# Third edge pass of a graph network: groups of edges taken in pairs

## The chip, the cores and the metric

The kernel runs on one core of one Trainium2 chip. The metric is the device time of one execution in microseconds (us). The core's engines work in parallel, each through its own list of instructions in order: PE (TensorE, matmuls), DVE (VectorE), ACT (ScalarE), POOL (GpSimd, which issues the gathers here) and SP (SyncE, which issues the plain loads). They wait for one another by semaphores. SBUF is the core's on-chip memory, PSUM the memory into which PE writes and from which DVE and ACT can read[...].

## The reference

A graph with 30,000 nodes of 128 features and 960,000 edges, sorted by destination, goes through two layers. The first is a relational convolution in two rounds; it takes the first and second pass over the edges. The second layer is the one that the change touches. For each of four edge types t:

```
k = x @ Wk[t] + bk[t];  q = x @ Wq[t] + bq[t];  v = x @ Wv[t] + bv[t]
eta = sigmoid(k[dst] + q[src])
msg = where(edge_type == t, eta * v[src], 0)
agg = segment_sum(msg, dst);  outs.append(agg + x @ Ws[t] + b[t])
```

and the layer's output is the mean over t, added to x. An edge has one type, so each edge needs one row k[dst, type], one q[src, type] and one v[src, type], one sigmoid and one product of 128 values, and a sum by destination. All is fp32.

## The kernel before, in words

The kernel makes three passes over the edges. The first two (functions named c1 and c2) compute the first layer; node tables for the second layer are made beside the second. Between and beside them, finished nodes are worked on in small steps. The third pass, named g, has its body in `gate_body`; only this function is changed.

A pass is a loop of 25 iterations (`NI`). An iteration has 100 groups (`NG`), a group three tiles of 128 edges (`G` = 3, `TP` = 128), five groups (`S`) are a superblock, and 25 groups a stage, for which the lists of source rows and of relative destinations are loaded at once (`loads`). As the edges are sorted, the destinations of a group lie in a window of 32 nodes.

The instructions stand on each engine as the program writes them (`manual_schedule`); nothing is reordered. For group n the third pass does this:

- `window(n)`, L555: SP loads 128 rows of the table of k that can occur in the group (`kw`, ten buffers, L560). It is called five groups ahead.
- `types(s)`, L551, and `onehot(s)`, L562: SP loads the codes of a superblock; DVE makes from them, by comparison, a one-hot matrix `oh` (128 x 1920, L564) that picks the row of k for each edge, and `sel` (128 x 480, L570) that picks the destination for each edge. `onehot(s + 1)` stands in group 1 of each superblock.
- `gather`, L118: POOL issues three indirect DMAs per group into `qv[n]`, each 128 rows of 256 values, q and v side by side. There are ten buffers of a group, so the gathers of group n wait until group n-10 has been used up.
- `keys(n)`, L574: three matmuls of `oh` and `kw` write k for 384 edges into `pk[n]`, one PSUM bank (four buffers).
- L618: DVE adds q to `pk[n]` in place; L619: ACT takes the sigmoid in place.
- `sums(n)`, L581: DVE multiplies `pk[n]` with v into `msg` (L586, three buffers); three matmuls (L588) sum the messages of the group by destination into `po[s]`.
- `add_windows`, L410 to L413: DVE adds the five windows of a superblock to the aggregate `agg` in SBUF. It stands in group 4 of the next superblock.
- `after_third`, L751 to L772: copies, transposes and stores finished nodes (`c`, `pr`, `o`).

The order within group n is: loads, gathers of n, `keys(n + 1)`, the addition and sigmoid of n, `sums(n - 2)`, and then, where they fall due, `onehot` and `add_windows`:

```
if n + 1 < NG:
    keys(n + 1)
nc.vector.tensor_add(pk[n], pk[n], qv[n][:, :, 0, :])
nc.scalar.activation(pk[n], pk[n], AF.Sigmoid)
if n > 1:
    sums(n - 2)
```

So on DVE the product of group n-2 comes directly behind the addition of group n, and PE alternates between three matmuls of keys and three of sums. The gathers of group n stand in POOL's list without any work of other engines between, so POOL can run ahead as far as the ten buffers of `qv` allow. At a stage's start, every 25 groups, `stage_boundary` stands in the program, and `leave_stage` ten groups later.

Of the kernel before, what the change touches and what calls it, by code (L numbers as in the profile page):

```python
# [9 lines left out]
F32 = mybir.dt.float32  # L10
I32 = mybir.dt.int32
BF16 = mybir.dt.bfloat16
AF = mybir.ActivationFunctionType
# [6 lines left out]
P = 128  # L20
D = 128
# [9 lines left out]
TP = 128  # L31
NT = E // TP
G = 3
GE = G * TP
W = 32
NGR = NT // G
S = 5
SB = 5
NQ = 4
NS = NQ * SB  # L40
NGS = S * SB
NTS = NGS * G
NG = S * NS
# [6 lines left out]
NX = N + LAG  # L50
LEAD = 3 * VB
GAP = 8
EPS = 1e-5
CH = 5
PX, KX = 120, 10
# [17 lines left out]
def kernel(  # L73
# [29 lines left out]
    nc = tc.nc  # L103
# [7 lines left out]
    qvtab = nc.dram_tensor("qvtab", (NX * T, 2 * D), F32, kind="Internal").ap()  # L111
# [5 lines left out]
    def gather(to, table, idx):  # L117
        nc.gpsimd.indirect_dma_start(  # L118
            out=to, out_offset=None, in_=table,
            in_offset=bass.IndirectOffsetOnAxis(ap=idx, axis=0))  # L120
# [23 lines left out]
    eps = consts.tile([P, 1], F32, name="eps")  # L144
    nc.vector.memset(eps, EPS)

# [188 lines left out]
    def sorted_path():  # L335
# [5 lines left out]
        with ExitStack() as all_:  # L341
# [40 lines left out]
            def leave_stage():  # L382

                for engine in ENGINES:
                    tc.previous_stage_wait(engine)

            def stage_tile(io, name, array, dt, i, k, more=0):

                t = io.tile([TP, NTS + more], dt, name=name)
                nc.sync.dma_start(t, array[:, ds(i * (NQ * NTS) + k * NTS, NTS + more)])  # L390
                return t

            def firsts(io, i, k):

                t = io.tile([1, 32], I32, name="firsts")
                nc.sync.dma_start(t, first_st[ds(i * NQ + k, 1), :])
                return t

            def bases(t, engine):
                _, vals = nc.values_load_multi_w_load_instructions(  # L400
                    t[:, :NGS], engines=[engine],
                    min_val=0, max_val=N - 1, skip_runtime_bounds_check_because=IN_RANGE)
                return vals

            def edge_row(row, i, s, n):

                return bass.AP(tensor=row.tensor, offset=(i * NG + s * S) * GE,
                               ap=[[0, n], [GE, S], [1, GE]])

            def add_windows(po, base, s):  # L410
                for g in range(S):
                    to = agg[:, ds(base[s % SB * S + g], W)]
                    nc.vector.tensor_add(to, to, po[:, g, :])  # L413
# [129 lines left out]
            def gate_body(i, io, pool, ps, cp, iw, ic, beside):  # L543
                stage = {}
                kb, oh, kw, sel, pk, qv, po, base, kbase = {}, {}, {}, {}, {}, {}, {}, {}, {}

                def loads(k):
                    stage[k] = [firsts(io, i, k)] + [stage_tile(io, *a, i, k) for a in (
                        ("qi", qidx, I32), ("relc", reld, F32))]

                def types(s):  # L551
                    kb[s] = pool.tile([P, S, GE], BF16, name="kb")
                    nc.sync.dma_start(kb[s], edge_row(kcode, i, s, P))

                def window(n):  # L555
                    k = n // NGS
                    if n % NGS == 0:
                        kbase[k] = bases(stage[k][0], SP)
                    kw[n] = pool.tile([P, D], F32, name="kw", bufs=10)
                    nc.sync.dma_start(kw[n], ktab[ds(kbase[k][n % NGS] * T, P), :])  # L560

                def onehot(s):  # L562
                    oh[s] = pool.tile([P, S, GE], F32, name="oh")
                    nc.vector.tensor_tensor(oh[s], kb[s],  # L564
                                            ic.unsqueeze(2).to_broadcast([P, S, GE]),
                                            ALU.is_equal)
                    sel[s] = pool.tile([TP, S * G, W], F32, name="sel", bufs=3)
                    t0 = s % SB * S * G
                    relc = stage[s // SB][2][:, t0:t0 + S * G]
                    nc.vector.tensor_tensor(  # L570
                        sel[s], iw[:TP].unsqueeze(1).to_broadcast([TP, S * G, W]),
                        relc.unsqueeze(2).to_broadcast([TP, S * G, W]), ALU.is_equal)

                def keys(n):  # L574
                    pk[n] = ps.tile([TP, G, D], F32, name="pk", bufs=4)
                    for j in range(G):
                        nc.tensor.matmul(pk[n][:, j, :],  # L577
                                         lhsT=oh[n // S][:, n % S, j * TP:(j + 1) * TP],
                                         rhs=kw[n], start=True, stop=True)

                def sums(n):  # L581
                    s, g = n // S, n % S
                    if g == 0:
                        po[s] = ps.tile([P, S, W], F32, name="po")
                    msg = pool.tile([TP, G, D], F32, name="msg", bufs=3)
                    nc.vector.tensor_mul(msg, pk[n], qv[n][:, :, 1, :])  # L586
                    for j in range(G):
                        nc.tensor.matmul(po[s][:, g, :], lhsT=msg[:, j, :],  # L588
                                         rhs=sel[s][:, g * G + j, :],
                                         start=(j == 0), stop=(j == G - 1))  # L590

                loads(0)
                types(0)
                for n in range(S):
                    window(n)
                onehot(0)
                keys(0)
                for n in range(NG):
                    s, g, k = n // S, n % S, n // NGS
                    if n % NGS == 0:  # L600
                        if n:
                            tc.stage_boundary()
                        if k + 1 < NQ:
                            loads(k + 1)
                    if g == 0 and s % SB == 2:
                        leave_stage()
                    if g == 0 and s + 1 < NS:
                        types(s + 1)
                    if n + S < NG:
                        window(n + S)  # L610
                    qv[n] = pool.tile([TP, G, 2, D], F32, name="qv", bufs=10)
                    t0 = n % NGS * G
                    for j in range(G):
                        gather(qv[n][:, j].rearrange("p a f -> p (a f)"), qvtab,
                               stage[k][1][:, t0 + j:t0 + j + 1])
                    if n + 1 < NG:
                        keys(n + 1)
                    nc.vector.tensor_add(pk[n], pk[n], qv[n][:, :, 0, :])  # L618
                    nc.scalar.activation(pk[n], pk[n], AF.Sigmoid)  # L619
                    if n > 1:  # L620
                        sums(n - 2)
                    if g == 1 and s + 1 < NS:
                        onehot(s + 1)
                    if g == 4 and s:
                        add_windows(po[s - 1], base[(s - 1) // SB], s - 1)
                    if g == 4 and s % SB == 0:
                        base[k] = bases(stage[k][0], DVE)
                    beside(n)
                sums(NG - 2)
                sums(NG - 1)  # L630
                add_windows(po[NS - 1], base[NQ - 1], NS - 1)


# [31 lines left out]
            def after_second(weights):  # L665
# [9 lines left out]
                def steps(at, pool, ps, deep):  # L675
# [6 lines left out]
                    hT = pool.tile([P, VB], F32, name="hT")  # L682
                    kt = pool.tile([VB, T, D + GAP], F32, name="kt")[:, :, :D]
                    qvt = pool.tile([VB, T, 2 * D + GAP], F32, name="qvt")[:, :, :2 * D]
                    got = {}
# [120 lines left out]
            edge_pass("c1", rel_body(h0, basis[0], False), after_first, 2, codes)  # L806
            edge_pass("c2", rel_body(h1, basis[1], True), after_second, 2)
            edge_pass("g", lambda weights: gate_body, after_third, 1)


# [230 lines left out]
```

## Time and profile before

| what | value |
|---|---|
| time, median of three runs | 33,966.85 us (33,952.1 to 33,968.91) |
| the profiled execution's own time | 34,363.18 us |
| its span, first to last instruction | 34,361.4 us |
| PE busy | 19,886.4 us, 58% |
| DVE busy | 12,399.5 us, 36% |
| ACT busy | 3,636.0 us, 11% |
| POOL busy | 21,304.2 us, 62% |
| third pass, from its first gather to its last | 22,630.1 to 34,330.1 us |
| granted TensorE clock, mean of the span | 0.675 |

The three passes compared, in stretches inside each of them (busy us):

| stretch | PE | DVE | ACT | POOL | clock | DMA share | GB/s |
|---|---|---|---|---|---|---|---|
| 200 to 11,500 | 6,415.79 | 3,933.95 | 1,009.46 | 7,063.54 | 0.74 | 0.24 | 64 |
| 11,600 to 22,500 | 6,587.65 | 4,036.69 | 1,160.89 | 7,005.11 | 0.78 | 0.25 | 65 |
| 22,700 to 34,300 | 6,679.37 | 4,180.45 | 1,318.54 | 7,022.93 | 0.51 | 0.41 | 122 |

How to read the lines of the profile that follow. A group row gives the line of the kernel, engine and operation, what it writes and reads, its shape and how often it occurs; then the busy time in us and the mean of one in ns; then how long the engine had been idle just before these instructions, with what ended most of that. A wait row names the engine and line, what ended the wait, its sum in us, how often, and the longest. A timeline row gives start and duration in us, the engine, the instruction, how many in a row it stands for (x), and in brackets the idle time ahead of it and what ended that. "issue" means that the profile shows nothing that the engine waited for, "remote" that the releaser is not among the instructions that the profile could name. Ends of matmuls are modelled, so the record of a matmul can end earlier than the matmul. The profile's own chain of the work that ended last is empty for this kernel.

### The profile page before, as it was taken

How to read it: one execution, taken by the hardware profiler on the slowest of the kernel's cores; microseconds unless marked ns; L12 is line 12 of the kernel's file. 1: busy time of each engine (PE TensorE's matmuls, PEld its weight loads, DVE VectorE, ACT ScalarE, POOL GpSimd, SP SyncE). 2: the span in 40 equal slices, each digit the busy share in tenths (PEclk: the TensorE clock that was granted, in tenths of full speed). 3: DMA queues.
4: the chain of work that ended last, by engine and by line, in shares of the span. 5: the costliest groups of instructions: out<-in, count | busy, mean ns of one | idle time of the engine just before them, and what ended most of it. 6: DMA issues, size and time to landing. Idle time of an engine off the chain costs nothing.

```text
span 34361.4 us, 321543 instructions
## 1 busy us (share of the span) xinstructions
PE 19886.4 (58%) x83304; PEld 16933.4 (49%) x83304; DVE 12399.5 (36%) x32695; ACT 3636.0 (11%) x9834; POOL 21304.2 (62%) x22514
## 2 busy tenths in 40 slices
PE   4555555555555566656656666555555555555555
PEld 3444444444444444444444444445555555555555
DVE  4333333333333333333333333333333333333333
ACT  1000000000000011111111111111111111111111
POOL 5666666666666666666666666656656666666665
PEclk7777777777777777777777777765555555555555
DMA  3222222222222222222222222234444444444443
GB/s 100 64 63 63 64 64 64 63 64 63 63 63 63 66 65 66 65 66 65 66 65 66 65 66 65 65 105 123 122 121 121 121 121 122 122 123 121 121 122 118
DMA packets 2171202, 2914.97 MB, mean 85 GB/s; under 512 B 684764, under 2 KB 1617880, under 8 KB 2169544
## 3 DMA queue, kind: packets, MB, share of 16 engines
q0 software_dynamic: 840000, 1967.52, 21.0%
q1 hardware_dynamic: 923347, 651.19, 6.5%
q10 hardware_dynamic: 406197, 276.11, 2.8%
q8 instruction: 802, 13.14, 0.2%
q14 instruction: 856, 7.01, 0.1%
HBM read 2618.79 MB, written 274.16 MB: 84 GB/s over the span
## 4 chain that ended last, share of the span: by engine, by line


## 5 line engine op out<-in xcount | busy, mean ns | idle before, releaser
L118 POOL DMA_INDIRECT hg<-h,idx x15000 | 14189.1, 946 | 8366.8 <-issue 4281.9
L520 PE MATMUL pa<-sb,hg 128*128 128x256 f32 x30000 | 9211.6, 464 | 6063.6 <-issue 3309.4
L520 PEld LDWEIGHTS pa<-sb,hg 128*128 128x128 f32 x30000 | 6897.0, 239 | 7881.0 <-issue 3785.8
L118 POOL DMA_INDIRECT qv<-qvtab,qi x7500 | 7088.1, 945 | 4658.3 <-issue 2317.6
L515 DVE SCALAR_TENSOR_TENSOR sb<-cp,relc,ce 128x256 f32<-128x256 f32 x15000 | 6132.8, 475 | 5165.4 <-remote 3864.0
L588 PE MATMUL po<-sel,msg 128*128 128x32 f32 x15000 | 3459.4, 387 | 4659.8 <-DVE msg L586 3274.0
L588 PEld LDWEIGHTS po<-sel,msg 128*128 128x128 f32 x15000 | 3417.7, 327 | 4956.1 <-DVE msg L586 3424.9
L577 PE MATMUL pk<-kw,oh 128*128 128x128 f32 x15000 | 3965.9, 438 | 332.2 <-DVE oh L564 284.4
L618 DVE TENSOR_TENSOR pk<-pk,qv 128x384 f32<-128x384 f32 x2500 | 1407.4, 563 | 7030.1 <-remote 5356.4
L524 ACT COPY ab<-pa 128x256 f32<-128x256 f32 x5000 | 1809.0, 373 | 20007.9 <-remote 10336.1
L577 PEld LDWEIGHTS pk<-kw,oh 128*128 128x128 f32 x15000 | 3460.6, 330 | 334.9 <-issue 334.9
L479 PE MATMUL po<-ab,bas 128*128 128x160 f32 x16000 | 2456.1, 308 | 275.1 <-ACT ab L524 144.6
L479 PEld LDWEIGHTS po<-ab,bas 128*128 128x128 f32 x16000 | 2381.7, 198 | 384.4 <-ACT ab L524 169.6
L413 DVE TENSOR_TENSOR agg<-agg,po 128x32 f32 x7500 | 1401.6, 187 | 2827.7 <-remote 699.9
L619 ACT ACTIVATE pk<-pk 128x384 f32<-128x384 f32 x2500 | 1185.8, 475 | 9327.1 <-DVE pk L618 5397.8
L715 PE MATMUL bank<-wall,hT 128*120 128x512 f32 x1524 | 1052.1, 814 | 1083.9 <-ACT hT L711 338.1
L586 DVE TENSOR_TENSOR msg<-pk,qv 128x384 f32<-128x384 f32 x2500 | 1368.1, 547 | 126.8 <-remote 94.6
L449 PE MATMUL cp<-coeff,oh 128*128 128x64 f32 x4000 | 693.9, 306 | 964.1 <-issue 769.6
L449 PEld LDWEIGHTS cp<-coeff,oh 128*128 128x128 f32 x4000 | 687.4, 233 | 1019.3 <-issue 902.4
L564 DVE TENSOR_TENSOR oh<-kb,cp 128x1920 f32<-128x1920 bf16 x500 | 1072.2, 2144 | 47.5 <-issue 31.9
L715 PEld LDWEIGHTS bank<-wall,hT 128*120 128x120 f32 x1524 | 346.5, 246 | 1429.1 <-issue 627.9
L726 DVE TENSOR_TENSOR kt<-bank,ball 120x512 f32<-120x512 f32 x254 | 175.7, 692 | 2336.7 <-PE bank L715 895.3
(77 smaller groups left out, 3396.7 us busy)
## 6 DMA issues: line engine op xcount, KB each, us to landing
hg<-h,idx POOLq DMA_INDIRECT x15000
kb<-kcode SPq DMA_DIRECT2D x500, 480.0 KB
kw<-ktab SPq DMA_DIRECT2D x2500, 64.0 KB
er<-in_et_row SPq DMA_DIRECT2D x2000, 64.0 KB
qvtab<-qvt ACTq DMA_DIRECT2D x254, 480.0 KB
qv<-qvtab,qi POOLq DMA_INDIRECT x7500
ktab<-kt ACTq DMA_DIRECT2D x254, 240.0 KB
ce<-ce ACTq DMA_DIRECT2D x500, 60.0 KB
```

The costliest lines, as they stand in the source:

```text
L118: nc.gpsimd.indirect_dma_start(out=to, out_offset=None, in_=table, in_offset=bass.IndirectOffsetOnAxis(ap=idx, axis=0))
L413: nc.vector.tensor_add(to, to, po[:, g, :])
L449: nc.tensor.matmul(pc[s][:, c].rearrange("p q l b -> p (q l b)"), lhsT=oh[s][:, c, :], rhs=coeff.rearrange("p q l b -> p (q l b)"), start= ...
L479: nc.tensor.matmul(po[s].rearrange("p s w -> p (s w)"), lhsT=bas[:, b, :], rhs=ab[s][:, b].rearrange("p s w -> p (s w)"), start=(b == 0), ...
L515: nc.vector.scalar_tensor_tensor(sb, iw[:TP].unsqueeze(1).to_broadcast([TP, B, W]), relc[:, t0 + j:t0 + j + 1], ce[s][:, g * G + j, :].uns ...
L520: nc.tensor.matmul(pa.rearrange("p b w -> p (b w)"), lhsT=hg[:, j, :], rhs=sb.rearrange("p b w -> p (b w)"), start=(j == 0), stop=(j == G ...
L524: nc.scalar.copy(ab[s][:, :, g, :], pa)
L577: nc.tensor.matmul(pk[n][:, j, :], lhsT=oh[n // S][:, n % S, j * TP:(j + 1) * TP], rhs=kw[n], start=True, stop=True)
L586: nc.vector.tensor_mul(msg, pk[n], qv[n][:, :, 1, :])
L588: nc.tensor.matmul(po[s][:, g, :], lhsT=msg[:, j, :], rhs=sel[s][:, g * G + j, :], start=(j == 0), stop=(j == G - 1))
L618: nc.vector.tensor_add(pk[n], pk[n], qv[n][:, :, 0, :])
L715: nc.tensor.matmul(bank(a, VB, T * D), lhsT=hT, rhs=wall[:, a].rearrange("p t f -> p (t f)"), start=True, stop=True)
```

## The change

Two neighbouring groups, n = 2m and 2m + 1, become a pair m. A pair's keys lie in one PSUM tile of two banks (`pk[m]`, two buffers[...]), its gathered rows in one `qv[m]` (five buffers of a pair), its messages in one `msg` (two buffers of a pair, by default of the pool). One addition, one sigmoid and one product work on the 768 values per partition of a pair. The matmuls and gathers stay as many; those of a pair's keys and of a pair's sums each stand together, six in a row.

The order changes too. In the second group of pair m the program has: `sums(m - 1)`, that is the product and the six matmuls of the pair before; then the keys of the next two groups; then the addition and the sigmoid of pair m. `onehot` and `add_windows` stay in groups 1 and 4 of their superblock. Windows of k are loaded seven groups ahead (`AHEAD`) and still have ten buffers. The stages begin at groups 0, 26, 50 and 76, so that a pair never crosses a boundary within the program's order, and a stage is left ten groups after it begins. The first two passes are the same.

```
--- before.py
+++ after.py
@@ -50,6 +50,7 @@
 NX = N + LAG
 LEAD = 3 * VB
 GAP = 8
+AHEAD = 7
 EPS = 1e-5
 CH = 5
 PX, KX = 120, 10
@@ -572,53 +573,62 @@
                         relc.unsqueeze(2).to_broadcast([TP, S * G, W]), ALU.is_equal)
 
                 def keys(n):
-                    pk[n] = ps.tile([TP, G, D], F32, name="pk", bufs=4)
+                    if n % 2 == 0:
+                        pk[n // 2] = ps.tile([TP, 2, 4, D], F32, name="pk")[:, :, :G, :]
                     for j in range(G):
-                        nc.tensor.matmul(pk[n][:, j, :],
+                        nc.tensor.matmul(pk[n // 2][:, n % 2, j, :],
                                          lhsT=oh[n // S][:, n % S, j * TP:(j + 1) * TP],
                                          rhs=kw[n], start=True, stop=True)
 
-                def sums(n):
-                    s, g = n // S, n % S
-                    if g == 0:
-                        po[s] = ps.tile([P, S, W], F32, name="po")
-                    msg = pool.tile([TP, G, D], F32, name="msg", bufs=3)
-                    nc.vector.tensor_mul(msg, pk[n], qv[n][:, :, 1, :])
-                    for j in range(G):
-                        nc.tensor.matmul(po[s][:, g, :], lhsT=msg[:, j, :],
-                                         rhs=sel[s][:, g * G + j, :],
-                                         start=(j == 0), stop=(j == G - 1))
-
+                def sums(m):
+
+                    msg = pool.tile([TP, 2, G, D], F32, name="msg")
+                    nc.vector.tensor_mul(msg, pk[m], qv[m][:, :, :, 1, :])
+                    for n in (2 * m, 2 * m + 1):
+                        s, g = n // S, n % S
+                        if g == 0:
+                            po[s] = ps.tile([P, S, W], F32, name="po")
+                        for j in range(G):
+                            nc.tensor.matmul(po[s][:, g, :], lhsT=msg[:, n % 2, j, :],
+                                             rhs=sel[s][:, g * G + j, :],
+                                             start=(j == 0), stop=(j == G - 1))
+
+                begins = [-(-k * NGS // 2) * 2 for k in range(NQ)]
                 loads(0)
                 types(0)
-                for n in range(S):
+                for n in range(AHEAD):
                     window(n)
                 onehot(0)
                 keys(0)
+                keys(1)
                 for n in range(NG):
                     s, g, k = n // S, n % S, n // NGS
-                    if n % NGS == 0:
+                    m = n // 2
+                    if n in begins:
                         if n:
                             tc.stage_boundary()
                         if k + 1 < NQ:
                             loads(k + 1)
-                    if g == 0 and s % SB == 2:
+                    if n - 2 * S in begins:
                         leave_stage()
                     if g == 0 and s + 1 < NS:
                         types(s + 1)
-                    if n + S < NG:
-                        window(n + S)
-                    qv[n] = pool.tile([TP, G, 2, D], F32, name="qv", bufs=10)
+                    if n + AHEAD < NG:
+                        window(n + AHEAD)
+                    if n % 2 == 0:
+                        qv[m] = pool.tile([TP, 2, G, 2, D], F32, name="qv", bufs=5)
                     t0 = n % NGS * G
                     for j in range(G):
-                        gather(qv[n][:, j].rearrange("p a f -> p (a f)"), qvtab,
+                        gather(qv[m][:, n % 2, j].rearrange("p a f -> p (a f)"), qvtab,
                                stage[k][1][:, t0 + j:t0 + j + 1])
-                    if n + 1 < NG:
-                        keys(n + 1)
-                    nc.vector.tensor_add(pk[n], pk[n], qv[n][:, :, 0, :])
-                    nc.scalar.activation(pk[n], pk[n], AF.Sigmoid)
-                    if n > 1:
-                        sums(n - 2)
+                    if n % 2:
+                        if m:
+                            sums(m - 1)
+                        if n + 2 < NG:
+                            keys(n + 1)
+                            keys(n + 2)
+                        nc.vector.tensor_add(pk[m], pk[m], qv[m][:, :, :, 0, :])
+                        nc.scalar.activation(pk[m], pk[m], AF.Sigmoid)
                     if g == 1 and s + 1 < NS:
                         onehot(s + 1)
                     if g == 4 and s:
@@ -626,8 +636,7 @@
                     if g == 4 and s % SB == 0:
                         base[k] = bases(stage[k][0], DVE)
                     beside(n)
-                sums(NG - 2)
-                sums(NG - 1)
+                sums(NG // 2 - 1)
                 add_windows(po[NS - 1], base[NQ - 1], NS - 1)
 
 
```

## The prediction, made before the change was run

> **What bounds the kernel now.** I began with the groups, by line. Each pass issues 7,500 gathers on POOL, and only the third is changed.
>
> ```profile
> L118 POOL DMA_INDIRECT qv<-qvtab,qi x7500 | 7088.1, 945 | 4658.3 <-issue 2317.6
> L618 DVE TENSOR_TENSOR pk<-pk,qv 128x384 f32<-128x384 f32 x2500 | 1407.4, 563 | 7030.1 <-remote 5356.4
> L619 ACT ACTIVATE pk<-pk 128x384 f32<-128x384 f32 x2500 | 1185.8, 475 | 9327.1 <-DVE pk L618 5397.8
> L586 DVE TENSOR_TENSOR msg<-pk,qv 128x384 f32<-128x384 f32 x2500 | 1368.1, 547 | 126.8 <-remote 94.6
> ```
>
> A gather takes 0.945 us and the next starts 0.30 us later, so three make a floor of 3.75 us per group. The third pass lasts from its first gather at 22630.1 to its last at 34330.1: 11,700 us, 4.68 per group. POOL's idle of 4658.3, less 7,500 x 0.30 = 2,250 and 46.5 for the first index load, leaves 2,362 us beyond the floor. The waits of POOL's queue in this pass say for what:
>
> ```profile
> POOL qv L118 <- issue: 2317.6, 6735, 4.4
> POOL qv L118 <- DVE msg L586: 1745.4, 486, 16.5
> POOL qv L118 <- DVE pk L618: 300.3, 102, 5.1
> POOL qv L118 <- DVE agg L413: 131.6, 60, 4.5
> POOL qv L118 <- ACT pk L619: 73.9, 16, 4.7
> ```
>
> Where the releaser is not msg, it stands beside msg on its engine. That is 664 waits (486 + 102 + 60 + 16), one in 3.8 groups. 25 of them, at the eleventh group of each iteration, are of 16.4 us: 25 x 16.1 = 402. The other 639 hold 2,362 - 402 = 1,960 us, 3.07 each beyond the 0.30, or 0.78 per group. Per group: 3.75 + 402/2,500 = 0.16 + 0.78 = 4.69, the measured pace. The timeline shows one such wait and the next stall of DVE:
>
> ```profile
> 28001.93 1.49 PE L577 MATMUL pk<-kw,oh 128*128 128x128 f32 x6
> ...
> 28005.68 0.95 POOL L118 DMA_INDIRECT qv<-qvtab,qi  x1 [0.30 <-issue]
> ...
> 28009.13 0.57 DVE L618 TENSOR_TENSOR pk<-pk,qv 128x384 f32<-128x384 f32 x1 [8.75 <-remote]
> 28009.61 0.55 DVE L586 TENSOR_TENSOR msg<-pk,qv 128x384 f32<-128x384 f32 x1
> ...
> 28010.42 0.94 POOL L118 DMA_INDIRECT qv<-qvtab,qi  x1 [3.79 <-DVE msg L586]
> ...
> 28013.63 0.56 DVE L618 TENSOR_TENSOR pk<-pk,qv 128x384 f32<-128x384 f32 x1
> ...
> 28016.17 0.57 DVE L618 TENSOR_TENSOR pk<-pk,qv 128x384 f32<-128x384 f32 x1 [1.53 <-PE po L588]
> ...
> 28025.39 0.57 DVE L618 TENSOR_TENSOR pk<-pk,qv 128x384 f32<-128x384 f32 x1 [8.20 <-remote]
> ...
> 28026.68 0.94 POOL L118 DMA_INDIRECT qv<-qvtab,qi  x1 [1.58 <-DVE msg L586]
> ```
>
> POOL runs out of free qv buffers and stops at 28006.63. DVE has waited for keys since long before, though PE's records of them had ended by 28003.4 and the gathers for this addition were issued about 30 us ago. 2.50 us after POOL's stop the addition goes, 0.48 later the product, 1.29 after the addition the first gather. The next additions are prompt up to 28016.17, 5.75 us after the restart; the one after that waits 8.20 us while POOL uses up the four groups released (12 gathers). So the third pass goes in rounds: a burst of about four groups of DVE work, their 15 us of gathers, a wait. What withholds keys from DVE while gathers stream I can't name; that it often yields when they pause I take from this view.
>
> [...] the pass runs at 0.51 on average, and matmuls back to back for 6.8 us stay at half before one window at full rate:
>
> ```profile
> 28036.27:28039.68 3.41, 3.41 (x17) 3.41 (x18) 2.22 (x5) 0.95 (x2) 2.50 (x4) 0.50 0.60 192
> 28039.68:28043.10 3.42, 3.42 (x17) 3.42 (x18) 0.00 (x0) 0.00 (x0) 2.66 (x3) 0.50 0.46 130
> 28043.10:28046.50 3.40, 0.41 (x4) 0.21 (x2) 0.40 (x1) 0.00 (x0) 2.64 (x3) 1.00 0.38 101
> ```
>
> (Columns: stretch, length, busy time of PE, weight load, DVE, ACT, POOL, then clock, DMA share, GB/s.)
>
> **The change, part by part.** *Fewer, longer operations.* 2,500 additions, products and sigmoids become 1,250 each of 768 elements. DVE's slope, from the 32-element row of L413 (187 ns) and the 384-element addition (563), is 1.07 ns per element: 0.97 us for the addition, 0.95 for the product. [...] Each pair saves 2 x 0.56 - 0.97 = 0.15, 0.14 and 0.15 us: 1,250 x 0.29 = 360 us of DVE and 190 of ACT. I count them as nothing: DVE is busy 36% of the span, and 0.80 us of the 9 us between 28016.4 and 28025.4. Without that cover they would be worth at most 360.
>
> *The chain that ends a wait.* Before, DVE goes from addition(n) straight to product(n-2), whose sigmoid is old, and that product frees the gathers: addition to product 0.48, product 0.55. After, the product that frees POOL is that of the pair just added: 0.97 + 0.80 + 0.95 = 2.72 against 1.03, or +1.69 us on every wait. Queued behind it on DVE are the next addition, one-hots and window sums; PE's sums wait for it.
>
> *What now stands between addition and product.* The one-hot pair of L564 and L570 (2.14 + 0.65 = 2.79 us) and the five window additions (1.07) were behind the product; both now come after a pair's addition and ahead of its product. Of 2.5 pairs in a superblock of five groups, one carries each. The sigmoid's 0.80 hides beneath, so the mean is (1.99 + 0.27)/2.5 = 0.9 us. Bounds: 0, if the late pair is never one of these, and 2.0, if it always is. The pair's phase shifts against the superblock, so I take the mean. A wait is then 3.07 + 1.69 + 0.9 = 5.66 us.
>
> *How many groups a round releases.* Before, two additions whose keys are done go at once, and two more come in the next 5.75 us, each behind 6 matmuls (2.56 us). After, two pairs go at once, as two pk buffers hold finished keys; a third needs 6 sums and 6 keys, 5.1 us from the first product, 4.9 after POOL's restart, just inside the prompt stretch. So six groups. A fourth pair needs 12 matmuls more, in the stretch in which 6 took 9.2 us (28016.17 to 28025.39): 18.4 from about 5, against 22.5 us of gathers. It comes at the end or too late; bounds 4 and 8.
>
> *Sum.* 5.66/6 = 0.94 per group against 0.78: +0.16 x 2,500 = +400 us. At an iteration's start POOL has filled all ten groups and waits for the first product. Before, one at 27835.91: keys from 27828.6, three additions and a one-hot pair, the product from 27835.09 to 27835.64. After: two groups of keys (2.56) to 27831.2, the addition to 27832.2, the one-hot pair to 27835.0, under which a table load (1.28) and the sigmoid fit, the product to 27835.9: +0.3 us x 25 = +10. Together +410 on the profiled execution (34,363, the span being 34,361, 1.2% above the median): 34,773, or 34,370 on the scale of the median.
>
> *The rest at nothing.* Gathers, loads, matmuls and their bytes stay as many. qv (5 pairs for 10) and pk (2 x 2 banks for 4 x 1) keep their size. msg, two pairs for three groups, is freed by PE's sums, a pair earlier. Windows are loaded two groups earlier in the program and still wait for the keys of ten groups before; the type rows behind them on SP's queue come five groups ahead of their one-hot. If that cover went, a load's time would be added per superblock. Stages begin one group later twice, once per 25 groups.
>
> **Rivals.** *A longer round* (faster): eight groups per wait, because six keys matmuls in a row bring the full clock more often, or the fourth pair comes in time. 5.66/8 = 0.71: -0.07 x 2,500 = -180 us; without the one-hot term 4.76/8 = 0.60: -460. So 33,790 to 33,510. For it: the 1.00 window above. Against: it followed two dense windows. It decides from 7.2 groups per wait (5.66/0.78). *POOL alone* (much faster): keys come promptly once DVE signals half as often, all ordinary waits go: -1,960, some 32,030. Against: the same pause before gathers exists in passes of other form (idle 8366.8 over 15,000, 0.26 us a gather beyond 0.30, against 0.31 here). *No change*: that same similarity may mean the pauses are paid per gather or per matmul, whatever DVE does: 33,967. *Four groups per round* (slower still): the third pair misses the prompt stretch; 5.66/4 = 1.42, +1,590, some 35,540. *Not what it says*: the operations cost double, not 1.7 times; 0.3 us per wait, inside the ranges.
>
> **How the numbers follow.** Six groups 0.50, longer rounds 0.22, POOL alone 0.08, no change 0.12, four groups 0.08. The likeliest gives 34,370; its own range runs from 34,000 (no one-hot term: 4.76/6 = 0.79) to 34,940 (half the waits after four groups: 1.18). The whole range is 33,500 to 35,000; it leaves out POOL alone, four groups and some edges. Slower by over 0.2%, about what a measurement here can tell: 0.57 (six groups less its edge, four groups). Within it: 0.13. Faster: 0.30.
>
> **What would show it.** Additions near 0.97 us, products 0.95, sigmoids 0.80. POOL's waits in the third pass: some 400 where there were 640, of about 6 us each. The gap from a late addition to POOL's restart: 3.0 us or, with a one-hot between, 5. Passes one and two as before. Wrong if the waits are not longer, if the rounds release eight groups or more, or if the pace is 3.9 us per group with hardly a wait.

## The result and the profile after

The kernel got slower: 34,699.85 us (34,682.82 to 34,755.36) against 33,967.88, a ratio of 1.0219 (95% interval 1.0205 to 1.0234). The forecast was 34,370, slower, with a range of 33,500 to 35,000. The increase of 732 us is nearly twice the forecast 400.

The groups by line, of the profile after (busy us and mean ns, then idle before and its main releaser):

```profile
L119 POOL DMA_INDIRECT qv<-qvtab,qi x7500 | 7088.7, 945 | 5181.1 <-DVE msg L586 2323.8
L630 DVE TENSOR_TENSOR pk<-pk,qv 128x768 f32<-128x768 f32 x1250 | 1203.2, 963 | 7561.6 <-remote 5950.8
L631 ACT ACTIVATE pk<-pk 128x768 f32<-128x768 f32 x1250 | 993.8, 795 | 9882.1 <-DVE pk L630 8678.9
L586 DVE TENSOR_TENSOR msg<-pk,qv 128x768 f32<-128x768 f32 x1250 | 1188.7, 951 | 396.9 <-ACT pk L631 228.0
```

The prices of the three operations came out as forecast: 0.963, 0.795 and 0.951 us. DVE saved 1,407.4 + 1,368.1 - 1,203.2 - 1,188.7 = 384 us and ACT 192, and neither shows in the time. POOL's idle went up instead, from 4,658.3 to 5,181.1 us. The waits of POOL's queue in the third pass:

```profile
POOL qv L119 <- DVE msg L586: 2300.2, 337, 15.8
POOL qv L119 <- issue: 2242.7, 6897, 7.4
POOL qv L119 <- DVE pk L630: 330.6, 43, 8.7
POOL qv L119 <- PE po L592: 180.1, 22, 8.7
```

There are 337 + 43 + 22 = 402 waits where there were 664, and a mean one has 7.0 us where it had 3.4. Between the starts of two successive waits longer than 0.8 us lie six groups in 396 of 425 cases. Before, it was four in 382 of 692. The timeline shows one round:

```profile
28010.67 0.97 DVE L630 TENSOR_TENSOR pk<-pk,qv 128x768 f32<-128x768 f32 x1 [17.29 <-remote]
28011.54 1.07 DVE L414 TENSOR_TENSOR agg<-agg,po 128x32 f32 x5
28011.67 0.80 ACT L631 ACTIVATE pk<-pk 128x768 f32<-128x768 f32 x1 [19.28 <-DVE pk L630]
28012.53 0.95 DVE L586 TENSOR_TENSOR msg<-pk,qv 128x768 f32<-128x768 f32 x1
...
28013.75 0.95 POOL L119 DMA_INDIRECT qv<-qvtab,qi  x1 [6.28 <-DVE msg L586]
...
28021.45 2.91 PE L579 MATMUL pk<-kw,oh 128*128 128x128 f32 x12
...
28031.39 0.37 PE L579 MATMUL pk<-kw,oh 128*128 128x128 f32 x1 [1.72 <-issue]
...
28033.49 0.37 PE L579 MATMUL pk<-kw,oh 128*128 128x128 f32 x1 [1.73 <-issue]
...
28039.29 0.97 DVE L630 TENSOR_TENSOR pk<-pk,qv 128x768 f32<-128x768 f32 x1 [17.41 <-remote]
28040.16 2.14 DVE L565 TENSOR_TENSOR oh<-kb,cp 128x1920 f32<-128x1920 bf16 x1
...
28042.79 0.95 DVE L586 TENSOR_TENSOR msg<-pk,qv 128x768 f32<-128x768 f32 x1
...
28044.62 0.94 POOL L119 DMA_INDIRECT qv<-qvtab,qi  x1 [8.70 <-DVE pk L630]
```

The addition at 28010.67 has waited 17.29 us. From its start to the product 1.86 us pass, with five window additions over the sigmoid; POOL restarts at 28013.75. In the next round the one-hot pair stands between: 3.50 us from addition to product, a wait of 8.70. The keys that the addition at 28039.29 waits for are those at 28021.45; their records had ended 15 us before. (A matmul of the program is two records: L579 has 15,000 for the 7,500 matmuls of 2,500 groups.) The single PE records from 28031.39 on, up to 2.1 us apart with nothing that PE waited for in the profile, are keys of the next pair.

The addition waits for PE's semaphore, and the trace has the times at which a semaphore was raised. Between 28024.4 and 28039.0 this one rose 3 times; from 28039.09 it rose 17 times within 0.7 us. So it is PE's signals that come late, and then in a burst. Over the 424 additions of the third pass that waited more than 4 us for PE, there were 0.38 rises per us during the wait, and 11.8 in the one microsecond around its end. (About a fifth of PE's rises are missing from this trace (the semaphore above rose 3,215 times for 4,000 instructions that raise it), so the counts are low; that the additions did wait is not in doubt.)

The third pass takes 12,225 us, from its first gather at 22,492.5 to its last at 34,717.4, where it took 11,699: +526. The two profiled executions differ by only 392 us (34,755 against 34,363), because in this one the first two passes, which the change leaves alone, took 138 us less. The medians differ by 732: the profiled execution before was 1.2% above its median, the one after 0.2%.

### The profile page after: what moved, and what is told of

It is laid out like the page before. It is cut to its first block, busy times and chain, and to the rows that moved or that the text cites. A ratio compares the mean times of both kernels' runs of the same rounds, so it can differ in the third digit from the quotient of the medians.

```text
span 34753.6 us, 314018 instructions
## 1 busy us (share of the span) xinstructions
PE 19157.6 (55%) x83304; PEld 16091.8 (46%) x83304; DVE 12218.1 (35%) x30195; ACT 3442.8 (10%) x8584; POOL 21300.3 (61%) x22514
## 4 chain that ended last, share of the span: by engine, by line
## 5 line engine op out<-in xcount | busy, mean ns | idle before, releaser
L119 POOL DMA_INDIRECT qv<-qvtab,qi x7500 | 7088.7, 945 | 5181.1 <-DVE msg L586 2323.8
L592 PE MATMUL po<-sel,msg 128*128 128x32 f32 x15000 | 2812.1, 352 | 4274.2 <-DVE msg L586 4163.5
L592 PEld LDWEIGHTS po<-sel,msg 128*128 128x128 f32 x15000 | 2785.7, 283 | 4574.7 <-DVE msg L586 4449.8
L579 PE MATMUL pk<-kw,oh 128*128 128x128 f32 x15000 | 3506.4, 385 | 1956.6 <-issue 1769.3
L579 PEld LDWEIGHTS pk<-kw,oh 128*128 128x128 f32 x15000 | 2983.9, 283 | 2060.1 <-issue 2053.0
L630 DVE TENSOR_TENSOR pk<-pk,qv 128x768 f32<-128x768 f32 x1250 | 1203.2, 963 | 7561.6 <-remote 5950.8
L631 ACT ACTIVATE pk<-pk 128x768 f32<-128x768 f32 x1250 | 993.8, 795 | 9882.1 <-DVE pk L630 8678.9
L724 PE MATMUL bank<-wall,hT 128*120 128x512 f32 x1524 | 1046.8, 810 | 948.8 <-DVE kt L735 321.3
L586 DVE TENSOR_TENSOR msg<-pk,qv 128x768 f32<-128x768 f32 x1250 | 1188.7, 951 | 396.9 <-ACT pk L631 228.0
L724 PEld LDWEIGHTS bank<-wall,hT 128*120 128x120 f32 x1524 | 352.7, 249 | 1293.3 <-issue 642.5
```

The lines of the kernel that those rows point to most:

```text
L119: nc.gpsimd.indirect_dma_start(out=to, out_offset=None, in_=table, in_offset=bass.IndirectOffsetOnAxis(ap=idx, axis=0))
L579: nc.tensor.matmul(pk[n // 2][:, n % 2, j, :], lhsT=oh[n // S][:, n % S, j * TP:(j + 1) * TP], rhs=kw[n], start=True, stop=True)
L586: nc.vector.tensor_mul(msg, pk[m], qv[m][:, :, :, 1, :])
L592: nc.tensor.matmul(po[s][:, g, :], lhsT=msg[:, n % 2, j, :], rhs=sel[s][:, g * G + j, :], start=(j == 0), stop=(j == G - 1))
L630: nc.vector.tensor_add(pk[m], pk[m], qv[m][:, :, :, 0, :])
L724: nc.tensor.matmul(bank(a, VB, T * D), lhsT=hT, rhs=wall[:, a].rearrange("p t f -> p (t f)"), start=True, stop=True)
```

## The experiments

My theory: POOL issues a round of gathers, runs out of buffers because the keys come late, and waits; each wait has the chain from the late addition to the product in it, and what counts is its length and how many groups a round releases. The runs were made in four rows, each on one chip and beside the kernel before. The kernel before took 34,307, 28,419, 34,412 and 34,381 us on them, so only ratios are compared across rows. In the first, third and fourth row keys come late, as on the chip of the forecast. The changed kernel was not in the first row; its ratio was 1.0219 and 1.0212 on two other chips with late keys, and the runs of the first row are compared with these.

**First row: the parts of the chain.** The one-hots and window additions moved ahead of the addition, from the changed kernel (`beside_dve` holds the lines taken out below):

```
 if m:
     sums(m - 1)
+for late in (n - 1, n):
+    beside_dve(late)
 if n + 2 < NG:
...
-if g == 1 and s + 1 < NS:
-    onehot(s + 1)
-if g == 4 and s:
-    add_windows(po[s - 1], base[(s - 1) // SB], s - 1)
```

> The changed kernel, with the one-hot pair and the window additions moved: in the second group of a pair, behind the product of the pair before and ahead of the addition, so that nothing stands between an addition and its own product but the sigmoid. Theory (each wait of POOL is lengthened by the chain addition, sigmoid, product, and by what stands in it): from addition to product 1.86 us in every wait in place of 2.65 on average, so 0.8 us x 426 waits = 340 us less than the changed kernel: about 34,360. Rival (one-hots are hidden, the length of the wait is set by when the keys come): no change from 34,700. Groups per wait stay six under both.

Measured 1.0134 (1.0117 to 1.0151), against 1.0212 for the changed kernel in the third row, on another chip: 0.8% less, some 270 us of the 340 forecast. Rounds stayed at six groups. From addition to product it is 1.83 us in every wait (2.66 in the mean before the move). The start of the addition after POOL's stop moved out by 0.0 to 0.5 us, depending on which of the two chips' profiles of the changed kernel one takes. The term is real.

The operations halved, from the changed kernel (product likewise, with `msg[:, h]`):

```
-nc.vector.tensor_add(pk[m], pk[m], qv[m][:, :, :, 0, :])
-nc.scalar.activation(pk[m], pk[m], AF.Sigmoid)
+for h in range(2):
+    nc.vector.tensor_add(pk[m][:, h], pk[m][:, h], qv[m][:, h, :, 0, :])
+    nc.scalar.activation(pk[m][:, h], pk[m][:, h], AF.Sigmoid)
```

> The changed kernel with pairs of buffers, keys and order kept, but the addition, the sigmoid and the product made for each group of a pair by itself (384 elements, two of each). Theory of the chain: the two groups overlap on DVE and ACT, so that the pair's product ends about 2.15 us after the start of its first addition and not 2.8; 0.6 us x 426 waits = 260 us less: about 34,440. Rival (DVE's time counts, and fewer, wider operations are a gain in themselves): 360 us more, about 35,060.

Measured 1.031 (1.0293 to 1.0327): slower than the changed kernel (1.0212) by 1.0%, near the rival's number. But its timeline shows another reason:

```profile
28014.11 0.57 DVE L632 TENSOR_TENSOR pk<-pk,qv 128x384 f32<-128x384 f32 x1 [15.23 <-PE pk L579]
28014.71 0.47 ACT L633 ACTIVATE pk<-pk 128x384 f32<-128x384 f32 x1 [18.86 <-DVE pk L632]
28015.21 0.57 DVE L632 TENSOR_TENSOR pk<-pk,qv 128x384 f32<-128x384 f32 x1 [0.54 <-ACT pk L633]
28015.69 1.07 DVE L414 TENSOR_TENSOR agg<-agg,po 128x32 f32 x5
...
28016.67 1.01 DVE L587 TENSOR_TENSOR msg<-pk,qv 128x384 f32<-128x384 f32 x2
```

The second half's addition waits for the first half's sigmoid, though the two halves share no values; both are parts of one tile. So the halves do not overlap as I assumed; the chain from the first addition to the end of the products became 3.57 us where the changed kernel, with the same window additions between, has 2.81. The third pass took 12,719 us, against 12,225 and 12,424 in the two profiles of the changed kernel in which keys come late, in rounds of six like theirs. The total alone does not tell DVE's time from the chain's, but the waits do. Against the profile of 12,424 us, from the third row and another chip, the time from POOL's stop to the addition is the same (3.42 and 3.40 us), and from there to the end of the pair's product it is 4.30 us in place of 3.62. Over 352 waits that is 240 us; the waits in the first ten groups of the iterations add 78. This covers the 294 us between the two passes and leaves nothing for DVE's time elsewhere.

The order alone, from the kernel before:

```
+if n:
+    sums(n - 1)
 if n + 1 < NG:
     keys(n + 1)
 nc.vector.tensor_add(pk[n], pk[n], qv[n][:, :, 0, :])
 nc.scalar.activation(pk[n], pk[n], AF.Sigmoid)
-if n > 1:
-    sums(n - 2)
```

> The kernel before with single groups throughout, and of the change only the order: the product and sums of group n-1 come first, then the keys of n+1, then the addition and sigmoid of n. Theory of the chain: 0.57 + 0.48 + 0.55 = 1.6 us from the late addition to the end of the product that frees POOL, against 1.03, and a one-hot pair between in one group of five (0.5 us in the mean): +1.1 us on some 640 waits, +700: about 34,670, as slow as the pairs. Rival (it is the pairing, the release of two groups at once or the wide operations, that costs): within 0.4% of 33,970.

Measured 1.0132 (1.0115 to 1.0149), +450 us of the 700 forecast: the order by itself, with single groups and nothing widened, gives 60% of the loss. Waits after the first ten groups of an iteration last 3.97 us in the mean (3.23 before), rounds have four groups most often, as before. A chain between the waits' two ends is thus enough to slow the kernel. It cost less than forecast although it grew as forecast (from addition to product 1.70 us, against 0.47 in the kernel before), because the addition came 0.47 us sooner after POOL's stop; why is not shown. The chain of the pairs is longer still, and their rounds are longer too.

Keys three ahead, from the kernel before; the one-hots and window additions, unchanged in themselves, stand between `sums` and `keys` (the windows, loaded seven groups ahead, and the first keys of an iteration are left out of the cut):

```
+if n:
+    sums(n - 1)
+if g == 1 and s + 1 < NS:
+    onehot(s + 1)
+if g == 4 and s:
+    add_windows(po[s - 1], base[(s - 1) // SB], s - 1)
-if n + 1 < NG:
-    keys(n + 1)
+if n + 3 < NG:
+    keys(n + 3)
 nc.vector.tensor_add(pk[n], pk[n], qv[n][:, :, 0, :])
 nc.scalar.activation(pk[n], pk[n], AF.Sigmoid)
-if n > 1:
-    sums(n - 2)
-if g == 1 and s + 1 < NS:
-    onehot(s + 1)
-if g == 4 and s:
-    add_windows(po[s - 1], base[(s - 1) // SB], s - 1)
```

> The kernel before with single groups, the product behind its own sigmoid as in the run of the order alone, the one-hots and window additions between product and next addition, and keys computed three groups ahead instead of one (four banks, as before), windows loaded seven ahead. Theory of rounds (a wait is paid once per round, so what counts is how many groups a round releases): three additions find finished keys at once and two or three more follow while keys are prompt, so six groups a round; the wait is 3.3 + 0.6 = 3.9 us, 3.6 beyond the 0.30, 0.60 per group against 0.78: 450 us less than before, about 33,500. Rival (the pauses are paid per gather or per matmul, however the groups are ordered): 33,970.

Measured 0.9915 (0.9898 to 0.9931): 290 us faster than the kernel before, of 450 forecast. Rounds have five or six groups (389 of 571), and the waits after the first ten groups are fewer, 492 in place of 632, and of 3.43 us in place of 3.23. It is the fastest version here against the kernel before. Its parts (keys ahead, order, place of the one-hots, windows) were not run apart.

**Second row: a chip without late keys.** The changed kernel again, the kernel before with 14 buffers, the changed kernel with fewer sums (told with the third row), and the three-ahead kernel with six message buffers.

> The changed kernel once more, beside the others of this row on one chip. Chips differ by about 1% (before took 33,970 us on one and 34,307 on the next), so the rows are compared by their ratio to before: 1.022 again if that ratio is the kernel's and not a chip's; the run with the one-hots ahead (1.013) then stands 0.9% below it.

> The kernel before with 14 buffers of gathered rows in place of 10, nothing else. Theory of rounds (a round releases as many groups as DVE and PE get through while keys are prompt, and that number does not depend on how far POOL is ahead): waits of the same number and length, four groups later in each iteration; ratio 1.000 within 0.003. Rival (the lateness of the keys grows with the look-ahead, or a longer look-ahead hides it): at least 1% up or down.

On this chip the kernel before took 28,419 us, and the changed one 28,418: ratio 1.0000 (0.9991 to 1.0009). POOL's waits in the third pass, of the changed kernel on this chip:

```profile
POOL qv L119 <- issue: 2219.4, 7279, 0.5
POOL qv L119 <- DMA qv<-qvtab,qi: 53.7, 172, 1.0
```

and the waits of its addition:

```profile
DVE pk L630 <- DMA qv<-qvtab,qi: 2764.2, 652, 6.4
DVE pk L630 <- PE pk L579: 1260.4, 312, 5.6
DVE pk L630 <- PE po L592: 687.7, 255, 3.4
```

No product holds POOL up; it goes at its floor, 3.76 us per group. The additions wait for the gathers more than for anything else, never over 6.4 us. PE's signals keep up: in the 179 waits of more than 4 us that PE ended, its semaphores rose 2.1 times per us, and no faster at the end. So neither the wide operations nor the longer chain costs anything where keys come in time. The 14 buffers could not answer their question here: 1.0053 (1.0036 to 1.007), by 24 waits of some 6.7 us at the iterations' first group, so the run says nothing of late keys. The fewer sums gave 1.0002 (0.9993 to 1.0011), the message buffers 0.9999 (0.9991 to 1.0008).

> The changed kernel with one matmul of sums per group in place of three; two thirds of the messages are left out of the sums. Theory (while gathers stream PE completes about one matmul per 1.5 us, so a pair's 12 matmuls decide when the next addition goes): with 8 per pair the fourth pair is ready about 17 us after POOL's restart, before six groups of gathers end at 22.5, so rounds of eight to ten groups; third pass about 4.4 us per group in place of 4.89, ratio to before about 0.985. Rival (gathers hold the keys back for as long as they stream, however few matmuls there are): rounds of six, ratio 1.02.

> The run with keys three groups ahead (ratio 0.9915), and six buffers of messages in place of three. In that run the product that ends a wait often waited 3.8 to 4.5 us itself, with its sigmoid done, and the only thing left for it was a buffer of messages, which PE's sums free. Theory: without that the products of three groups go one behind the other as soon as the keys come, rounds become longer, some 200 us less: 0.985. Rival (the product waits for nothing but the release of PE's earlier matmuls, which the next addition needs too): 0.9915 again.

**Third row: late keys again.**

> The changed kernel a third time. In the row before, on a chip where the kernel before took 28,419 us, it took as long as before within 0.1%, POOL issued gathers without a pause and no keys came late; on the first chip the ratio was 1.022. Theory (the change costs time only where keys are withheld while gathers stream, so that POOL runs dry, and this differs between chips): 1.020 to 1.024 if the kernel before takes about 34,000 here, 1.000 if it takes about 28,400. Rival (1.022 belongs to one chip): some other ratio at 34,000. In the first case it is the missing companion of the first row: one-hots ahead 1.0134, single operations 1.031, order alone 1.0132, so these stand 0.9% below, 0.9% above and 0.9% below it.

Measured 1.0212 (1.0195 to 1.023): the loss came back as on the first chip, again with six groups in 397 of 422 rounds. The fewer sums, from the changed kernel:

```
-for j in range(G):
+for j in range(1):
     nc.tensor.matmul(po[s][:, g, :], lhsT=msg[:, n % 2, j, :],
                      rhs=sel[s][:, g * G + j, :],
-                     start=(j == 0), stop=(j == G - 1))
+                     start=True, stop=True)
```

> The changed kernel with one matmul of sums per group in place of three (two thirds of the messages are left out of the sums), again, for a chip on which keys come late. If while gathers stream PE completes about one matmul per 1.5 us, a pair's matmuls decide when the next addition goes: 8 per pair in place of 12 give rounds of eight to ten groups, and a ratio of about 0.985. If gathers hold the keys back for as long as they stream, however few matmuls there are: rounds of six, 1.02. On a chip without late keys: 1.000.

Measured 1.0072 (1.0052 to 1.0092), between the two numbers. What the theory said of rounds came about: eight groups in 244 of 354 cases. What it said of time did not, as the waits did not get shorter.

```profile
POOL qv L119 <- DVE msg L586: 2034.1, 264, 11.6
POOL qv L119 <- issue: 2327.7, 7030, 7.4
POOL qv L119 <- DVE pk L630: 444.1, 73, 10.0
```

These 337 waits, the two rows of DVE, are of 7.4 us, and the 400 of the changed kernel on this chip, counted likewise, are of 7.5. So fewer matmuls per pair do let a round release more groups, and I had the gain of it too high. My "one matmul per 1.5 us" had counted records, of which a matmul has two. Nor does the lateness come from the pace at which PE starts its matmuls: here the records of a pair's keys start within 2.5 us of each other in 95% of the long waits (over 4 us), and yet the addition went 19.5 us (median) after the last of them, and 15.4 in the changed kernel on this chip.

Six message buffers, one line on top of the three-ahead kernel:

```
-msg = pool.tile([TP, G, D], F32, name="msg", bufs=3)
+msg = pool.tile([TP, G, D], F32, name="msg", bufs=6)
```

> Keys three groups ahead, product directly behind its own sigmoid, one-hots between product and next addition, and six buffers of messages, again, for a chip on which keys come late. If the products that waited 3.8 to 4.5 us waited for message buffers alone: about 0.985 of before. If for PE's earlier matmuls, which the next addition needs too: 0.9915, as with three buffers. On a chip without late keys: 1.000.

Measured 0.9966 (0.9953 to 0.9978): neither number; set against the 0.9915 of the first row, on another chip, the extra buffers took back part of the gain. Waits after an iteration's start fell from 492 to 417, but a mean one grew from 3.43 to 4.53 us. So more buffers of messages did not bring the time that I expected of them. Why the waits grew was not settled.

**Fourth row: half the bytes.** The kernel before with the lines below, and with q in the place of v in the product:

```
-qv[n] = pool.tile([TP, G, 2, D], F32, name="qv", bufs=10)
+qv[n] = pool.tile([TP, G, 1, D], F32, name="qv", bufs=10)
...
-    gather(qv[n][:, j].rearrange("p a f -> p (a f)"), qvtab,
+    gather(qv[n][:, j].rearrange("p a f -> p (a f)"),
+           qvtab.rearrange("n (a f) -> (n a) f", a=2),
```

> The kernel before, with gathers of half rows in the third pass: as many gathers and rows, but 128 values of each row in place of 256; v is left out and q stands in its place in the product. If it is the bytes that the gathers move that hold the keys back, the waits of POOL fall by about half: third pass 4.3 us per group in place of 4.68 to 4.7, ratio about 0.97 where before takes about 34,000. If it is the gathers as such (their number, or their rows): 1.00 within 0.005. On a chip without late keys: 1.000, as POOL issues as many.

Measured 0.9985 (0.9978 to 0.9992). The rate in the third pass fell from 122 to 80 GB/s, the last figure of this stretch:

```profile
22800.00:34200.00 11400.00, 6580.27 (x29597) 6294.16 (x29597) 4122.57 (x8315) 1307.07 (x2961) 6922.10 (x7338) 0.51 0.29 80
```

and the pace stayed at 4.66 us per group, in rounds of four. PE's semaphores rose 0.41 times per us during the long waits, against 0.42 in the kernel before. The bytes that the gathers move do not hold the keys back.

## Why the prediction was right, and where its sizes were off

**What bounds the kernel: right on this chip.** Rounds of four groups in the kernel before, of six in the changed one, are in the traces. The prediction rested on keys being late while gathers stream and left the cause open. In its own timeline it took the wrong records: those up to 28003.4 are the next group's, and those of the late addition had ended at 28000.76, 8.4 us before it (its gathers were issued 36 us before, not 30). The traces show what is late, PE's signals. Why, the runs leave open: they exclude the bytes of the gathers, and the granted clock, which in the third pass of the changed kernel was 0.59 here and 0.60 on the chip without late keys; and they show that it varies from chip to chip.

**The chain: right to a few hundredths.** In the waits after an iteration's first ten groups, from the late addition to its product it was 0.47 us before and 2.66 after, +2.19; the forecast was 0.97 + 0.80 + 0.9 - 0.48 = 2.19. The product grew by 0.40, as forecast. The one-hot pair stood between in 35% of the waits (forecast: one pair in 2.5). The addition took 963 ns and the product 951, where the slope of DVE in the profile before gave 970 and 950. The sigmoid took 795 ns, 320 more than at 384 elements; no row of the profile before shows the forecast's 0.80. ACT's copies there come near it: 373 ns at 256 elements (L524) and 594 at 512 (L724) rise by 0.86 ns per element, which from 475 gives an estimate of 806.

**Groups per round: right.** Six. The rivals with eight, with four, and with no wait did not come about in this kernel; the granted clock was a little higher (mean 0.59 in the third pass, 0.51 before) without making rounds longer. "No change" is what the chip without late keys does; on the forecast's chip it was wrong.

**The step that was mis-sized: the wait before the chain.** "A wait is then 3.07 + 1.69 + 0.9 = 5.66 us" takes over the time from POOL's stop to the late addition. That part grew from 1.86 to 2.94 us, and to 3.40 in the third row's profile of the changed kernel, so a wait came to 6.59 and 7.08 beyond the 0.30. Why is not shown: a pair has twice the matmuls behind one addition, but the run with fewer sums, in which a pair has a third fewer, had 3.62 there, beside the 3.40 on the same chip. The sum by the runs: outside an iteration's first ten groups before 632 waits x 2.93 = 1,852 us, after 356 x 6.59 = 2,346, so +494; at the start +47, where I had +10; the small gaps took back 16. Together the 526 us of the third pass, against a forecast of 410.

**The scale.** I divided the sum by 1.012, because the profiled execution before lay so far above the median. The execution after did not (0.2%), and so 526 us in the profiles stand against 732 in the medians. The first two passes, which are the same program, tell why this comparison falls short: they took 22,630 us in the profile before, 22,493 in the one after, and 22,637 to 22,687 in all profiles of the first, third and fourth row, where the kernel before took 34,307 to 34,412. The profile before thus has the pace of those chips. Set against the third row's profile of the changed kernel (22,687), the third pass grew from 11,699 to 12,425, by 725 us: 353 waits x 7.08 = 2,499, so +647 outside the first ten groups, and +70 at the start. That is the loss that the medians show, and the mis-sized step has then 1.54 us on every wait. On which chip the profile before was taken is not on record, so this stays likely, not shown.

**The range.** It ran from 1.4% faster to 3% slower, and the prediction gave "slower" 0.57. That the time lies inside says little; the number of groups per round and the growth of the chain say more.

**The operations at nothing: right.** 384 us of DVE and 192 of ACT were saved. Where keys come in time the ratio was 1.0000 with them saved; where keys come late, the run with single operations lost no more than its waits lost.

## What to carry to other kernels

Here an engine in the loop was idle two thirds of the time, joining its instructions saved nothing, and the joined instructions gave their result back later. In such a case look for what the last instruction of the chain releases, and count from the thing that arrives late to that release, with everything that stands between on the same engine. A wait that is paid once per round is judged by two numbers, its length and the work that a round releases; the version with keys three groups ahead raised the second with waits hardly longer (3.43 us against 3.23) and won 0.85%. And a loss or gain of this kind may exist only where the late thing is late: measure it on more than one chip.

## What the runs showed of the hardware that was not expected

The same program, the kernel before, took 33,968, 34,307, 34,412 and 34,381 us in four of the five rows of runs (the one of the result included) and 28,419 in the fifth, a sixth less. Gathers took as long there (0.947 us to issue against 0.945, and 1.5 us from then to the data's landing in the median, on both kinds of chip), but keys never came late: PE's semaphores rose 2.1 times per us during the additions' long waits for PE. Halving the bytes of the third pass's gathers changed 0.15% where keys come late, so what holds the keys back is not the volume that these gathers move. What differs between the chips, these runs don't tell.

In the four slower rows PE's signals fall behind its records while gathers stream: by 15.4 us in the median of the third row's long waits; by at least 3.03 us in the first row before the addition at 28019.99 of the order alone, which had waited 7.01 us; in the fourth row PE's semaphores rose 0.41 times per us. In the changed kernel they come in a burst some 3 us after the gathers stop: 0.38 rises per us during the long waits, 11.8 in the microsecond at their end. A view of waits then names no releaser ("remote"), as the matmul's record ended long before, by 15 us in the median in the changed kernel.

In the run with single operations a second half's addition waited for the first half's sigmoid in 1,128 of 1,250 pairs, 0.54 us in the median, though the halves share no values. Both halves are parts of one tile; whether that is the cause was not shown, as no run had them in two.
